# Two expert layers as seven block products, with the sums on VectorE and GpSimd and the scatters re-ordered

## The chip, the cores and the metric

The kernel runs on one core of a Trainium2 chip. The metric is device time in microseconds for one execution. TensorE (PE) multiplies and writes to PSUM; VectorE (DVE) and ScalarE (ACT) read PSUM and SBUF; GpSimd (POOL) works in SBUF and issues the indirect transfers; SyncE (SP) issues most other transfers.

## What is computed

A block of several stages on x of 4 x 512 tokens with 256 channels, all in float32. Only the first stage matters here, a mixture of experts: each token goes to the two of 8 experts that its gate ranks highest, and each expert is three matrix products.

```python
gate_w = softmax(xn @ wg_W + wg_b + (genre_embed @ gg_W + gg_b))
topk_w, topk_i = top_k(gate_w, 2)
h1 = relu(x @ W1[e] + b1[e])       # 256 -> 512
h2 = relu(h1 @ W2[e] + b2[e])      # 512 -> 512
out_e = h2 @ W3[e] + b3[e]         # 512 -> 256
moe = sum over the two experts of weight * out_e
```

The result goes through a blockwise linear attention, is added to x, and then passes a second attention and two feed-forward layers, none of which the diff touches but for one sum.

## The kernel before

**Stages.** The gate (lines 1206 to 1406) ranks the experts, counts the tokens of each and gives each token-expert pair a row in a list of slots. A slot has one expert and 256 rows (a pair of tiles) or 128 (a half slot); `SLOTS` (line 38) lists 24 of them, in the order 1,2,2 / 1,2,2 / 1,2,2,2 (three times) / 1,2,2 / 1 / 1,1, the figure being the number of 128-row tiles. The last two are inside a conditional; the other 22 (`often`, 15 pairs and 7 half slots) always run. `rowtok` holds each row's token and `goal` the row of the DRAM table `ys` where its result goes; empty rows have goal 0.

**The expert loop** (lines 1506 to 1525) does one slot j per pass, in this program order: layer 1 of slot j; the last layer of slot j - 1 (`last`, line 1477), its bias sum into `ob` and its scatters; the loads of the next slot's weights (`loads`, 1429: w1 with the biases 516 KB, w2 1 MB, w3 640 KB, double buffered); the gathers of its tokens and their transposes (`gather`, 1440, transposes at line 86 by the name `pxb`); one weight for a later stage; layer 2 of slot j. `layer` (1458) makes for each block of 128 output channels a product over 2 or 4 blocks of 128 inputs, with the 256 (or 128) tokens as the moving operand, into PSUM tiles `ph`; the relu with bias that takes them out (`relu`, 1418) goes to ACT and DVE in turn. All matmuls are issued by one helper, so they carry line 82 and are told apart by tile names: `ph` for the first two layers, `po` for the last.

**What orders the work.** A scheduler orders each engine's instructions by priority and its own estimates, and puts in all waits; instructions given to `keep_in_program_order` (`pinned`, line 1203, and `PE.in_order`) keep their order among themselves on their engine. Before the change only the transposes in `gather` are pinned in this loop, so GpSimd's other work may move in front: the sums xres + bo of the linear attention stage (line 1579, four of 128 x 1024) depend on nothing of the experts.

[...]

**After the loop** `conditions` (a small chain of another stage) fills gaps, `results` (1543) reads `ys` back, `weighted` (1554) makes y of each batch from the two expert results with ACT and then DVE (line 1558, tile `ymoe`), and `front` (1574) transposes y and begins the attention.

## Time and profile before

| | us |
|---|---|
| median of 3 runs | 1364.95 (1364.46 to 1367.05) |
| the profiled execution, its own time | 1364.1 |
| its span, first to last instruction | 1362.3 |
| expert loop in it, first layer product to last evacuation | 42.7 to 313.8 |

| in the expert loop | busy us |
|---|---|
| PE | 269.2 |
| DVE | 57.9 |
| ACT | 43.2 |
| POOL | 76.2 |

The span is what the trace covers; a run's time holds 1.8 us more around it. The profile names an operation by line, engine, and output<-input tiles. Busy time is what an engine's instructions cover, and "idle before" what it stood still ahead of them, with the instruction that ended the wait. PE is the matmul side and PEld the loading of weight blocks, which runs beside it. A float32 product shows as two records on each.

### The profile page before, as it was taken

What the parts mean: (1) busy time and instruction counts of PE and PEld (TensorE: products, weight loads), DVE (VectorE), ACT (ScalarE), POOL (GpSimd) and SP (SyncE); (2) the same over time, 40 slices, a digit from 0 to 9 for tenths busy, and PEclk for the clock granted to TensorE, in tenths of its full rate; (3) what the DMA queues carried; (4) which work ended last, traced back from release to release, by engine and by line L of the source; (5) the groups of instructions that cost most, each with busy time, mean ns of one, the idle gap of its engine ahead of it and who ended that gap; (6) DMA issues with size and microseconds to landing.
All of it is one profiled execution on the core that took longest, in us unless ns stands there. A gap on an engine that the chain in (4) does not pass through costs nothing.

```text
span 1362.3 us, 25766 instructions
## 1 busy us (share of the span) xinstructions
PE 1302.8 (96%) x10700; PEld 850.1 (62%) x10700; DVE 645.4 (47%) x1343; ACT 563.9 (41%) x1111; POOL 227.1 (17%) x223
## 2 busy tenths in 40 slices
PE   5899999998999999999999999999999998999998
PEld 4788888884666644444435665766555566667654
DVE  6222212125777743332226777764362767765421
ACT  4111111125555456565655646552223565463111
POOL 1324322211000020010103322100030312210010
PEclk7999999999999999999999999999999999999999
DMA  4577666644000000000201011211001011011000
GB/s 135 205 244 280 228 231 240 211 155 136 1 1 1 0 1 1 1 0 1 90 5 67 13 29 37 81 42 25 24 1 43 24 34 26 19 42 50 20 20 26
DMA packets 43110, 95.02 MB, mean 70 GB/s; under 512 B 9568, under 2 KB 25192, under 8 KB 40168
## 3 DMA queue, kind: packets, MB, share of 16 engines
q1 hardware_dynamic: 37560, 81.81, 18.1%
q0 software_dynamic: 3792, 10.24, 2.2%
q8 instruction: 88, 1.44, 0.4%
q10 hardware_dynamic: 1632, 1.21, 0.3%
q14 instruction: 38, 0.31, 0.1%
HBM read 83.95 MB, written 7.21 MB: 67 GB/s over the span
## 4 chain that ended last, share of the span: by engine, by line
PE 83%; DVE 7%; ACT 6%; issue 2%; DMA 1%; POOL 0%; POOLq 0%; SPq 0%; DVEq 0%; ACTq 0%
PE ph L82 14%; PE pdq L82 10%; PE sc L82 6%; PE pfy L82 6%; PE pug L82 5%; PE pua L82 5%; PE pv L82 5%; PE po L82 5%; PE pdy L82 4%; PE pn L82 3%; PE pz L82 2%; PE pds L82 2%; ACT p L685 2%; PE pqk L82 1%; PE pur L82 1%
## 5 line engine op out<-in xcount | busy, mean ns | idle before, releaser
L82 PE MATMUL pdq<-wqkv,yT 128*128 128x512 f32 x384 | 171.2, 596 | 6.0 <-ACT yT L613 4.1
L425 ACT ACTIVATE cex<-sc 128x512 f32<-128x512 f32 x256 | 131.8, 607 | 84.5 <-PE sc L82 84.4
L82 PE MATMUL ph<-h,w 128*128 128x256 f32 (+1 forms) x704 | 132.8, 346 | 1.6 <-DVE h L1422 1.6
L639 POOL TENSOR_TENSOR qr<-t,t 128x512 f32<-128x512 f32 x64 | 81.3, 1271 | 297.4 <-DVE t L636 282.8
L82 PEld LDWEIGHTS pdq<-wqkv,yT 128*128 128x128 f32 x384 | 71.4, 190 | 90.3 <-issue 76.9
L82 PEld LDWEIGHTS ph<-h,w 128*128 128x128 f32 x704 | 116.1, 191 | 13.7 <-DVE h L1422 1.9
L1420 ACT ACTIVATE h<-ph,w 128x256 f32<-128x256 f32 (+1 forms) x88 | 35.3, 437 | 190.9 <-PE ph L82 130.5
L1422 DVE TENSOR_SCALAR h<-ph,w 128x256 f32<-128x256 f32 (+1 forms) x88 | 36.1, 438 | 161.1 <-PE ph L82 102.6
L685 ACT ACTIVATE p<-pds,ss 128x192 f32<-128x192 f32 (+1 forms) x256 | 82.3, 434 | 12.5 <-PE pds L82 11.2
L82 PE MATMUL sc<-qm,kT 32*128 32x512 f32 x512 | 86.8, 639 | 0.0
L629 ACT ACTIVATE sq<-pdq 128x512 f32<-128x512 f32 x64 | 38.4, 601 | 97.1 <-POOL qr L639 50.2
L82 PE MATMUL pug<-hT,w 128*128 128x512 f32 x160 | 75.9, 597 | 0.0
L82 PE MATMUL pua<-hT,w 128*128 128x512 f32 x160 | 75.2, 592 | 0.0
L82 PE MATMUL ph<-xbT,w 128*128 128x256 f32 (+1 forms) x352 | 68.7, 347 | 0.5 <-ACT xbT L127 0.5
L82 PE MATMUL po<-w,h 128*128 128x256 f32 x296 | 67.6, 379 | 0.0
L395 POOL TENSOR_SCALAR fterm<-vw,faT 128x256 f32<-128x256 f32 x16 | 14.6, 922 | 312.1 <-DVE cr L385 259.6
L789 ACT ACTIVATE gl<-pug,cols 128x512 f32<-128x512 f32 x40 | 27.3, 687 | 86.5 <-PE pug L82 86.4
L82 PEld LDWEIGHTS ph<-xbT,w 128*128 128x128 f32 x352 | 58.5, 191 | 7.2 <-ACT xbT L127 0.7
L82 PE MATMUL pfy<-w,uA 128*128 128x256 f32 x256 | 61.2, 382 | 0.0
L82 PEld LDWEIGHTS pn<-p,v 64*64 64x64 f32 x1792 | 44.1, 136 | 27.4 <-issue 10.1
L82 PE MATMUL pv<-cex,v 128*32 128x512 f32 x512 | 61.2, 597 | 0.0
L82 PEld LDWEIGHTS po<-w,h 128*128 128x128 f32 x296 | 55.7, 190 | 8.1 <-ACT h L1420 0.9
(304 smaller groups left out, 2182.7 us busy)
## 6 DMA issues: line engine op xcount, KB each, us to landing
w<-in_moe_w_dram SPq DMA_DIRECT2D x22, 1024.0 KB
w<-in_moe_w_dram SPq DMA_DIRECT2D x22, 640.0 KB
w<-in_moe_w_dram SPq DMA_DIRECT2D x22, 516.0 KB
zb<-rows SPq DMA_DIRECT2D x32, 256.0 KB
g<-ys SPq DMA_DIRECT2D x6, 512.0 KB
wqkv<-in_f_wqkv_dram SPq DMA_DIRECT2D x2, 1536.0 KB
w<-in_f_w_dram SPq DMA_DIRECT2D x2, 1408.0 KB
out_dram<-yc SPq DMA_DIRECT2D x16, 128.0 KB
```

What stands on the lines that cost most here:

```text
L82: cls._queue(nc.tensor.matmul(*args, **kw))
L395: nc.gpsimd.tensor_scalar_mul(fterm[:, t, :], vw, W["faT"][:, t, b : b + 1])
L425: nc.scalar.activation(ex[:, i, :], pss[2 * j + i], AF.Exp, scale=CHD**-0.5)
L629: nc.scalar.activation(sq, p3, AF.Square)
L639: nc.gpsimd.tensor_tensor(qr_t[:, s], t1, t2, ALU.add)
L685: nc.scalar.activation(p[:, at : at + n], pss[j // 2][r][:, at % 384 : at % 384 + n], AF.Exp, scale=d.ss[:, j, 1, 2 * c + r : 2 * c + r + 1])
L789: nc.scalar.activation(gl, pg, AF.Gelu, bias=col("bg", l * (NU + 1) + i))
L1420: nc.scalar.activation(dst, src, AF.Relu, bias=bias)
L1422: nc.vector.tensor_scalar(dst, src, bias, 0.0, ALU.add, ALU.max)
```

## The change

For the pairs from slot 2 on (`few`, 14 of the 15), the first two layers are no longer made in eight block products. Weights, tokens and results are cut into 2 x 2 blocks; seven products of blocks or of sums of blocks (`layer_few`) give the same four result blocks after further sums, the scheme known from Strassen and Winograd. In detail:

- Each product has 128 tokens as moving operand and 256 output channels (2 matmul calls in layer 1, 4 in layer 2).
- GpSimd makes four sums of weight blocks per layer (`first_sums` of 256 columns, `second_sums` of 512), kept in the unused output tiles of the stage.
- DVE makes four sums of token blocks per layer (`token_sums`), always with one operand in PSUM: for layer 1 from the transposes' bank, for layer 2 from a second copy of h1's blocks that ACT writes into two PSUM banks (`both_banks`).
- DVE adds the products into result blocks (`plus`, seven per layer); all relus of these slots are on ACT, per 128 x 128 block.
- The slot's order changes: gathers (`fetch`) go two slots ahead; the two scatters of a pair are issued half a slot apart (the second one in the next pass, behind layer 1); nearly all instructions of the loop are pinned.
- Empty rows get a row of `ys` of their own (128 rows more, `maside`) instead of row 0, and rowtok is made ahead of goal.
- The banks are 4 `mm`, 1 `tp`, 1 `acc`, 2 for the copies; one gate product moves to `mm`.
- The sums of line 1579 are pinned, and so stay behind the scatters on GpSimd.

The diff, cut to its core (the constants' extra column, pins without other change, and the conditional slots' calls are left out):

```diff
-            moe.enter_context(banks("ps0", mm=4, tp=2, acc=2))
+            moe.enter_context(banks("ps0", mm=4, tp=1, acc=1, act=2))
...
-            ys = dr.tile([1 + 2 * B * S, H], F32, tag="ys", name="ys")
+            ys = dr.tile([1 + 2 * B * S + 128, H], F32, tag="ys", name="ys")
...
-            goal = xp.tile([128, NROWT], I32, tag="goal", name="goal")
-            nc.vector.tensor_copy(goal, pmap2[:, :NROWT])
+            goalf = xp.tile([128, NROWT], F32, tag="goalf", name="goalf")
+            nc.vector.scalar_tensor_tensor(goalf, pmap2[:, :NROWT], 0.0, maside.to_broadcast([128, NROWT]),
+                                           ALU.is_equal, ALU.mult)
+            goal = xp.tile([128, NROWT], I32, tag="goal", name="goal")
+            nc.vector.tensor_tensor(goal, pmap2[:, :NROWT], goalf, ALU.add)
...
-            def gather(j, d):
-                xb = hp.tile([128, 2, H], F32, tag="xb", name="xb", bufs=3)
+            def fetch(j, d):
+                d.xb = hp.tile([128, 2, H], F32, tag="xb", name="xb", bufs=3)
                 for i in range(d.n):
                     r = place(d.n, SLOTS[j][0]) + i
-                    nc.gpsimd.indirect_dma_start(
-                        out=xb[:, i, :], out_offset=None, in_=xall,
-                        in_offset=bass.IndirectOffsetOnAxis(ap=rowtok[:, r : r + 1], axis=0))
+                    pinned(nc.gpsimd.indirect_dma_start(
+                        out=d.xb[:, i, :], out_offset=None, in_=xall,
+                        in_offset=bass.IndirectOffsetOnAxis(ap=rowtok[:, r : r + 1], axis=0)))
+
+            def turn_tokens(d):
                 n = d.n * 128
                 pt = tpt("pxb")
-                with PE.in_order():
-                    for c in range(2):
-                        for i in range(d.n):
-                            PE.transpose(pt[:, c * n + i * 128 : c * n + (i + 1) * 128],
-                                         xb[:, i, c * 128 : (c + 1) * 128], ident)
-                xbT = hp.tile([128, 2, 256], F32, tag="xbT", name="xbT")
-                evac(xbT[:, :, 0:n], pt[:, : 2 * n].rearrange("p (c t) -> p c t", t=n))
-                d.xbT = xbT
+                for c in range(2):
+                    for i in range(d.n):
+                        PE.transpose(pt[:, c * n + i * 128 : c * n + (i + 1) * 128],
+                                     d.xb[:, i, c * 128 : (c + 1) * 128], ident)
+                d.xbT = hp.tile([128, 2, 256], F32, tag="xbT", name="xbT")
+                dst, src = d.xbT[:, :, 0:n], pt[:, : 2 * n].rearrange("p (c t) -> p c t", t=n)
+                pinned(nc.scalar.copy(dst, src))
+                if d.few:
+                    d.t1 = token_sums(d.xbT, src)
 
...
+            spare = [r.rearrange("p t h -> p (t h)") for r in y]
+            sums1 = spare[0].rearrange("p (k c m) -> p k c m", k=4, c=1)
+            sums2 = [r.rearrange("p (k c m) -> p k c m", k=2, c=2) for r in spare[1:3]]
+            sums2 = [sums2[k // 2][:, k % 2] for k in range(4)]
+
+            def first_sums(d):
+                d.s1 = [sums1[:, k] for k in range(4)]
+                weight_sums(d.s1, d.w1[:, 8:].rearrange("p (c m) -> p c m", m=ME))
+
+            def second_sums(d):
+                d.s2 = sums2
+                weight_sums(d.s2, d.w2)
+
+            def weight_sums(s, w):
+                n = w.shape[1] // 2
+                a11, a12, a21, a22 = (w[:, j0 * n : (j0 + 1) * n, 256 * i0 : 256 * i0 + 256]
+                                      for i0 in range(2) for j0 in range(2))
+                pinned(nc.gpsimd.tensor_tensor(s[0], a21, a22, ALU.add))
+                pinned(nc.gpsimd.tensor_tensor(s[1], s[0], a11, ALU.subtract))
+                pinned(nc.gpsimd.tensor_tensor(s[2], a11, a21, ALU.subtract))
+                pinned(nc.gpsimd.tensor_tensor(s[3], a12, s[1], ALU.subtract))
+
+            def token_sums(src, psum=None):
+                n = src.shape[1] // 2
+
+                def blocks(of):
+                    return [of[:, i0 * n : (i0 + 1) * n, 128 * j0 : 128 * j0 + 128]
+                            for i0 in range(2) for j0 in range(2)]
+
+                b11, b12, b21, b22 = blocks(src)
+                _, c12, c21, c22 = blocks(src if psum is None else psum)
+                if n == 1:
+                    t = hp.tile([128, 4, 1, 128], F32, tag="t1", name="t1", bufs=1)
+                else:
+                    t = spare[3].rearrange("p (k c t) -> p k c t", k=4, c=2)
+                pinned(nc.vector.tensor_tensor(t[:, 0], c12, b11, ALU.subtract))
+                pinned(nc.vector.tensor_tensor(t[:, 1], c22, t[:, 0], ALU.subtract))
+                pinned(nc.vector.tensor_tensor(t[:, 2], c22, b12, ALU.subtract))
+                pinned(nc.vector.tensor_tensor(t[:, 3], c21, t[:, 1], ALU.subtract))
+                return t
+
+            def both_banks():
+                return ps_now["pool"].tile([128, 4, 256], F32, tag="act", name="ph1", bufs=1)
+
+            def layer_few(d, src, t, tag, w, s, bias, copies=None):
+                n = w.shape[1] // 2
+                dst = hp.tile([128, 4, 256], F32, tag=tag, name=tag)
+                e1, e15, e16, e17 = (
+                    hp.tile([128, 2, 128], F32, tag=nm, name=nm, bufs=1) for nm in ("e1", "e15", "e16", "e17"))
+
+                def whole(i0, j0):
+                    return [[w[:, j0 * n + c, 256 * i0 + 128 * m : 256 * i0 + 128 * m + 128] for c in range(n)]
+                            for m in range(2)]
+
+                def summed(k):
+                    return [[s[k][:, c, 128 * m : 128 * m + 128] for c in range(n)] for m in range(2)]
+
+                def product(lhs, rhs):
+                    ps = mmt("ph")[:, :256].rearrange("p (m t) -> p m t", t=128)
+                    for m in range(2):
+                        mm(ps[:, m], [(lhs[m][c], rhs[:, c]) for c in range(n)])
+                    return ps
+
+                def block(i0, j0, out, p, other):
+                    plus(out, p, other)
+                    for m in range(2):
+                        pinned(nc.scalar.activation(
+                            dst[:, 2 * i0 + m, 128 * j0 : 128 * j0 + 128], out[:, m], AF.Relu,
+                            bias=d.w1[:, bias + 2 * i0 + m : bias + 2 * i0 + m + 1]))
+                    if copies is not None and (i0, j0) != (0, 0):
+                        for m in range(2):
+                            pinned(nc.scalar.activation(
+                                copies[:, 2 * i0 + m, 128 * j0 : 128 * j0 + 128], out[:, m], AF.Relu,
+                                bias=d.w1[:, bias + 2 * i0 + m : bias + 2 * i0 + m + 1]))
+
+                def plus(out, p, other):
+                    pinned(nc.vector.tensor_tensor(out, p, other, ALU.add))
+
+                p1 = product(whole(0, 0), src[:, 0:n, 0:128])
+                pinned(nc.scalar.copy(e1, p1))
+                p2 = product(whole(0, 1), src[:, n : 2 * n, 0:128])
+                block(0, 0, e15, p2, e1)
+                p6 = product(summed(1), t[:, 1])
+                plus(e16, p6, e1)
+                p5 = product(summed(0), t[:, 0])
+                plus(e15, p5, e16)
+                p7 = product(summed(2), t[:, 2])
+                plus(e17, p7, e16)
+                block(1, 1, e16, p5, e17)
+                p4 = product(whole(1, 1), t[:, 3])
+                block(1, 0, e1, p4, e17)
+                p3 = product(summed(3), src[:, n : 2 * n, 128:256])
+                block(0, 1, e15, p3, e15)
+                return dst
+
...
             def last(j, d):
                 ps = acct("po")
                 for i in range(d.n):
                     mm(ps[:, i * H : (i + 1) * H],
                        [(d.h2[:, c, i * 128 : (i + 1) * 128], d.w3[:, c, :]) for c in range(4)])
                 ob = hp.tile([128, 2, H], F32, tag="ob", name="ob", bufs=3)
-                nc.vector.tensor_tensor(
+                pinned(nc.vector.tensor_tensor(
                     ob[:, 0 : d.n, :], ps[:, : d.n * H].rearrange("p (i h) -> p i h", h=H),
-                    d.w3[:, 4, :].unsqueeze(1).to_broadcast([128, d.n, H]), ALU.add)
-                for i in range(d.n):
+                    d.w3[:, 4, :].unsqueeze(1).to_broadcast([128, d.n, H]), ALU.add))
+                d.ob = ob
+
+            def scatter(j, d, i):
+                if i < d.n:
                     r = place(d.n, SLOTS[j][0]) + i
-                    nc.gpsimd.indirect_dma_start(
+                    pinned(nc.gpsimd.indirect_dma_start(
                         out=ys, out_offset=bass.IndirectOffsetOnAxis(ap=goal[:, r : r + 1], axis=0),
-                        in_=ob[:, i, :], in_offset=None)
+                        in_=d.ob[:, i, :], in_offset=None))
 
 
...
-            ds = [SimpleNamespace() for _ in SLOTS]
+            ds = [SimpleNamespace(few=n == 2 and j > 1) for j, (_, n) in enumerate(SLOTS)]
+            for d, (_, d.n) in zip(ds, SLOTS):
+                pass
             loads(0, ds[0])
-            gather(0, ds[0])
+            fetch(0, ds[0])
+            fetch(1, ds[1])
+            with PE.in_order():
+                turn_tokens(ds[0])
             often, rare = ds[:-NRARE], range(len(ds) - NRARE, len(ds))
             for j, d in enumerate(often):
                 if j == len(often) - 1:
@@ -1511,18 +1620,40 @@
                     halves = nc.values_load(nhalf[0:1, 0:1], min_val=0, max_val=2 * NE)
                 if j == 1:
                     weights()
-                h1 = layer(d, d.xbT, "h1", d.w1[:, 8:].rearrange("p (c m) -> p c m", m=ME), 0)
-                if j:
-                    last(j - 1, ds[j - 1])
-                if j + 1 < len(often):
-                    loads(j + 1, ds[j + 1])
-                    gather(j + 1, ds[j + 1])
-                    if j > 1 and later:
-                        name, behind[0] = next(iter(later)), True
-                        cw_[name] = later.pop(name)()
-                        behind[0] = False
-                d.h2 = layer(d, h1, "h2", d.w2, 4)
+                w1 = d.w1[:, 8:].rearrange("p (c m) -> p c m", m=ME)
+                after = ds[j + 1] if j + 1 < len(often) else SimpleNamespace(few=False)
+                with PE.in_order():
+                    if d.few:
+                        copies = both_banks()
+                        h1 = layer_few(d, d.xbT, d.t1, "h1", w1, d.s1, 0, copies)
+                        t2 = token_sums(h1, copies)
+                    else:
+                        h1 = layer(d, d.xbT, "h1", w1, 0)
+                    if j + 1 < len(often):
+                        loads(j + 1, after)
+                        if later and j > 1:
+                            name, behind[0] = next(iter(later)), True
+                            cw_[name] = later.pop(name)()
+                            behind[0] = False
+                    if j > 1:
+                        scatter(j - 2, ds[j - 2], 1)
+                    if after.few:
+                        first_sums(after)
+                    if j + 2 < len(often):
+                        fetch(j + 2, ds[j + 2])
+                    if j:
+                        last(j - 1, ds[j - 1])
+                        scatter(j - 1, ds[j - 1], 0)
+                        if j == len(often) - 1:
+                            scatter(j - 1, ds[j - 1], 1)
+                    if j + 1 < len(often):
+                        turn_tokens(after)
+                    d.h2 = layer_few(d, h1, t2, "h2", d.w2, d.s2, 4) if d.few else layer(d, h1, "h2", d.w2, 4)
+                if after.few:
+                    second_sums(after)
             last(len(often) - 1, often[-1])
+            for i in range(2):
+                scatter(len(often) - 1, often[-1], i)
 
...
-                nc.gpsimd.tensor_tensor(
-                    xres[b], xres[b], row("bo").unsqueeze(1).to_broadcast([128, NT, H]), ALU.add)
+                pinned(nc.gpsimd.tensor_tensor(
+                    xres[b], xres[b], row("bo").unsqueeze(1).to_broadcast([128, NT, H]), ALU.add))
```

## The prediction

> **What bounds the kernel now.** First the page: is any engine full?
>
> ```profile
> span 1362.3 us, 25766 instructions
> ...
> PE 1302.8 (96%) x10700; PEld 850.1 (62%) x10700; DVE 645.4 (47%) x1343; ACT 563.9 (41%) x1111; POOL 227.1 (17%) x223
> ```
>
> TensorE is, over the whole span. The change touches the expert stage only, so next come the busy times of the stretch from its first matmul to its last evacuation (columns: sum; then PE, weight loads, DVE, ACT, POOL with counts; clock, DMA share, GB/s), and TensorE's waits there (total, times, longest).
>
> ```profile
> 42.70:313.80 271.10, 269.16 (x1441) 239.14 (x1442) 57.91 (x132) 43.18 (x102) 76.23 (x75) 1.00 0.62 217
> ```
> ```profile
> PE ph L82 <- DVE h L1422: 1.6, 1, 1.6
> PE pxb L86 <- DMA xb<-in_x_dram,rowtok: 1.2, 1, 1.2
> PE ph L82 <- ACT xbT L127: 0.5, 1, 0.5
> ```
>
> PE works 269 of 271 us at full clock and waits once each, all at the start. DVE, ACT and POOL have 200 us free. Here a matmul removed is time removed, as long as nothing new waits. The chain that ended last gives the prices (start, us, what, records):
>
> ```profile
> 106.35 8.69 PE ph L82 x48
> 115.04 3.46 PE po L82 x16
> ...
> 118.94 7.03 PE ph L82 x48
> 125.97 1.73 PE po L82 x8
> 127.69 0.44 PE pxb L86 x4
> 128.13 10.36 PE ph L82 x48
> ```
>
> Each matmul call leaves two records (a slot's last layer has 8 calls, and `po` x16). 10.36/48 = 0.216 us for 256 columns. 8.69 is 32 such records and 16 of a half slot, whose records have 128 columns: (8.69 - 32 x 0.216)/16 = 0.111; 7.03 is the reverse mix: (7.03 - 16 x 0.216)/32 = 0.112. So half the columns cost 52%.
>
> **What is saved.** A 256-row slot has 8 + 16 calls, 48 records, 10.36 us. Seven products instead of eight make 14 + 28 calls of 128 columns, 84 records x 0.1117 = 9.38 us. Saved: 0.98 us, in 14 slots (the second slot, j = 1, stays), 13.7 us. [...] The row decides: the half slots, loading full blocks for every 128 columns, take 0.112, so the loads are hidden.
>
> **What is added to GpSimd.** Rows by shape:
>
> ```profile
> L639 POOL TENSOR_TENSOR qr<-t,t 128x512 f32<-128x512 f32 x64 | 81.3, 1271 | 297.4 <-DVE t L636 282.8 <-PE pdy L82 13.5 <-PE pds L82 1.0
> L1488 POOL DMA_INDIRECT ys<-ob,goal x37 | 36.5, 987 | 101.0 <-DMA ys<-ob,goal 53.9 <-DVE ob L1483 31.5 <-issue 8.5
> ...
> L1483 DVE TENSOR_TENSOR ob<-po,w 128x256 f32<-128x256 f32 x7 | 3.0, 425 | 8.6 <-PE po L82 8.6
> ```
>
> Weight sums: 4 of 512 columns x 1.27, and 4 of 256 x 0.725 (row L396) = 8.0 us per slot. Its two gathers and two scatters, 0.98 each with 0.3 between, are 5.1. Per round of half, pair, pair, pair GpSimd has 3 x 8.0 + 7 x 2.56 = 42 us. TensorE's round, from the chain: half 9.3, first pair 12.5 - 1, later pairs 14.3 - 1 each, 47.4. So 89% full, with this order of dues: while a half slot runs (9.3 us), GpSimd needs w1 of the next slot, issued 1.2 us in and landing about 3.5 us later (1-us stretches: 300 GB/s); first sums done at 7.7, due 10.2 (its third product); two gathers and a scatter to 11.5; second sums' needed one at 14, due 16.4. They are hidden with 2 us to spare. Scatters wait for the one before (53.9 us over 16 waits in row L1488, 3.4 each); the new spacing puts 5 us of sums or gathers between them, and what was an idle queue now has sums, gathers and scatters behind each wait. I take nothing; 2 us of slack per round is the cover.
>
> **What is added to DVE and ACT, and the wait that comes of it.** DVE: 14 block sums x 0.43, token sums, about 9.5 us per slot; ACT: 22 relus and two copies, 7. Neither is full, but their chain is long: layer 2's third product needs the token sums of h1, whose first needs the last block's relu and copy. The pace of ACT and the interplay of DVE with GpSimd are read here:
>
> ```profile
> 29.59 1.06 ACT L1390 ACTIVATE ol<-ol,mc 128x64 f32<-128x64 f32 x4 [8.63 <-DVE ol L1381]
> ...
> 744.46 2.49 ACT L685 ACTIVATE p<-pds,ss 128x192 f32<-128x192 f32 x8
> ```
> ```profile
> 322.44 2.34 POOL L1579 TENSOR_TENSOR xres<-xres,crows 128x1024 f32<-128x1024 f32 x1 [5.20 <-DMA g<-ys]
> 322.84 2.62 DVE L1558 SCALAR_TENSOR_TENSOR ymoe<-g,m,g 128x256 f32<-128x256 f32 x2 [0.37 <-ACT g L1557]
> ```
> ```profile
> 1144.85 2.40 POOL L775 TENSOR_TENSOR yc<-yc,drows 128x1024 f32<-128x1024 f32 x1 [3.38 <-DVE hn L762]
> ...
> 1145.47 5.08 DVE L732 TENSOR_TENSOR oT<-oT,zb 128x512 f32<-128x512 f32 x2
> ...
> 1147.33 2.67 POOL L778 TENSOR_TENSOR yc<-yc,xres 128x1024 f32<-128x1024 f32 x1
> ```
>
> Back to back, ACT takes (1.06 - 0.34)/3 = 0.24 us for 64 columns and (2.49 - 0.43)/7 = 0.29 for 192; for 128 between them, 0.27 (it was never seen alone back to back; unpipelined it is 0.37, row L1420). From the start of layer 1 of a slot, TensorE's products end every 0.45 us, to 3.12. ACT is still in the relus of the slot before, so the first copy e1 ends at 1.65 (after a half slot 1.8, whose four relus take turns to 1.8); DVE then sums: 2.1, 2.4, 3.2 (waits for the first block's relu), 3.6, and block 11 at 4.0. From there 12 ACTs x 0.27 + 0.1 end at 7.4, two token sums x 0.43 at 8.3. TensorE's cover: 3.12, then the last layer of the slot before, 3.46 (after a half slot only 1.73), transposes 0.44, and two products of layer 2, 1.79: due at 8.8, after a half slot at 7.1. So a slot after a slot (9 cases) doesn't wait, with 0.5 spare; a slot after a half slot (5 cases: j = 4, 7, 11, 15, 19) waits 8.4 - 7.1 = 1.3. Cost 6.5 us (5.0 at pace 0.24; at 0.37 it is 2.5 x 5 and 0.6 x 9, 18 us). The output's sum, and with it the scatter, sits behind the token sums on DVE, 2.5 us later than now; its readers, GpSimd and later TensorE's bank, have that much. Four product banks: the fifth product of layer 1 needs e1 (1.65 against 1.79), the sixth block 00 (2.13 against 2.23), the seventh 2.46 against 2.68. No wait if exact, 0.2 if not: I take 0.07 x 14 = 1.0 (0 to 4).
>
> **What is moved: the residual sums.** Three of the four L1579 sums run at 127.6 to 134.6 in the expert stage, beside DVE work with a PSUM input, at no cost. Pinned, they queue behind the scatters and run right after the one shown, at 324.8 to 332. In that row two DVE operations with both inputs in SBUF take 2.62 us instead of 0.9: DVE stood still until the POOL sum ended. With two POOL sums back to back (1144.85, 1147.33), two took 5.08 instead of 1.3: one gets through per POOL sum. (Where one input is PSUM nothing happens: a DVE row at 895.66 takes its usual 0.74 beside a POOL sum. The new DVE sums all have a PSUM input, so I charge them nothing.) So the fourth ymoe piece of batch 0, on which the transposes wait, comes after the second POOL sum, 2.5 us later; batch 1's pieces then delay a copy by little. Their own readers (the tail sums, first at 395) are 60 us off. Cost 2.5 us (0 if the scheduler spreads them, 5 if batch 1's pieces hold qk's copy a full sum).
>
> The rest: goal's two operations go behind rowtok, 0.1 us gained (first used by the scatter at 58.0, made at 37; without that cover 0.4). Gathers go two slots ahead, so they wait for no transposes; on SP the loads keep their order, w3 still behind the last layer of the slot before. The regrouped gate banks are free microseconds before they are taken (the position sums' bank is last read at 26.0, taken again at 30.4; if not, some 0.3 each); conditions' small DVE chain behind busier queues at j = 21, 0 to 1, taken as 0.
>
> **Sum**, against the profiled execution (1364.1, span 1362.3, 0.85 below the median 1364.95): -13.7 + 6.5 + 1.0 + 2.5 = -3.7 us. Median 1361.2, say 1361.
>
> **Rivals.**
> - *The full saving* (20%): ACT's pace hides the token sums, or DVE and ACT overlap better; only the moved sums cost: -13.7 + 2.5 = -11, 1354. For it: the half-slot wait is only 1.3 against a chain I priced step by step. Against it: twelve ACTs on one chain.
> - *GpSimd becomes the bound* (20%): slower. Its 42 us per round meet 47.4 at a 22% higher price of a sum (1.55 us instead of 1.27), or with one scatter landing wait of 3.4 per slot. At 1.9 us a sum (12 per slot): GpSimd 54 against 47.4, 6.7 x 3 rounds plus some 3 x 2 in the shorter ones, 26 - 13.7 + 2.5 = +15, 1380; with scatter waits of 2 per slot in the full rounds only, about +3, 1368. For it: 89% leaves little, and every step waits in program order. Against it: row L639's 64 sums all take 1.27 beside a busy DVE.
> - *ACT's chain at 0.37* (12%): +18 in place of +6.5, +8, slower, 1373.
> - The change does nothing: no; 14 slots must show 128-column records.
>
> The forecast has 48%, within -7 to 0. What a measurement can tell from no change is 0.2%, 2.7 us. Faster: 20 and 33 of the 48; same: 14 of it; slower: 20 + 12 and the last 1: 53, 14, 33. Range 1353 to 1373: it leaves out the far end of the GpSimd case.
>
> **What would show it.** Right: 128x128 records at 0.112; in `ph` groups 84 records per slot; PE waits of some 1.3 us on DVE token sums just in the five slots after a half; ymoe rows stretched beside four POOL sums near 310 to 325. Wrong: PE waiting for POOL sums (the bound has moved), for DVE in every slot, or record intervals over 0.12.

## The result, and the profile after

The changed kernel takes 1378.0 us (median of 4, 1376.2 to 1378.7) where the kernel before takes 1365.5 (median of 4): 1.0085 times as long, 95% interval 1.007 to 1.010. On another chip it was 1.0102 (1.0076 to 1.0128). The forecast was 1361. In the profiled executions the span grew by 14.5 us, from 1362.3 to 1376.8.

First the head of the page.

```profile
span 1376.8 us, 27515 instructions
...
PE 1302.3 (95%) x11204; PEld 862.5 (63%) x11204; DVE 727.4 (53%) x1585; ACT 652.7 (47%) x1402; POOL 337.7 (25%) x335
```

TensorE is busy as long as before (1302.3 against 1302.8 us). Matmul work was saved and something took its place. The busy times of the expert stage (columns as before), and TensorE's waits in it:

```profile
44.66:318.68 274.02, 263.74 (x1945) 246.56 (x1946) 134.06 (x373) 131.77 (x392) 177.66 (x182) 0.99 0.64 215
```
```profile
PE ph L82 <- DVE ymoe L1519: 7.5, 10, 1.4
PE ph L82 <- ACT e L1562: 0.8, 5, 0.2
PE ph L82 <- ACT xbT L1460: 0.5, 1, 0.5
PE pcs L82 <- DVE hdT L244: 0.4, 1, 0.4
PE pfp L82 <- DVE hdT L244: 0.4, 1, 0.4
```

Before, TensorE was busy for 269.2 of 271.1 us. Now it is 263.7 of 274.0: its busy time shrank by 5.4 us. That is less than 13.7: 1.7 us of work was lost to a lower clock, and waits of a few tenths count as busy, since the profile shows a 128-column record as 0.28 us long where records start 0.11 apart. Its idle time grew from 1.9 to 10.3. The wait the forecast named, for the token sums (L1519), leads the list.

Where the 14.5 us arose, from TensorE's timelines of both profiles (each row runs from the start of the item in the row before; the pair of profiles is one execution each):

| from ... to | before, us | after, us | difference | forecast |
|---|---|---|---|---|
| start ... last layer of slot 0 | 54.2 | 54.8 | +0.6 | -0.1 |
| ... last layer of slot 19 | 234.3 | 236.2 | +1.9 | -5.6 |
| ... last layer of slot 20, with the conditions | 14.7 | 17.0 | +2.3 | -0.6 |
| ... first product of q and k | 23.5 | 25.6 | +2.1 | with the next row +2.5 |
| ... first scores of the attention stage | 14.6 | 17.9 | +3.3 | |
| ... end | 1021.0 | 1025.2 | +4.2 | 0 |

The difference runs through two things at once, idle time and clock. Summing (1 - granted clock) x TensorE's busy time over 2-us stretches gives the work lost to a reduced clock: 6.3 us in the profile before, 14.7 in the one after, so 8.4 of the 14.5. (More on this at the end: part of it is luck of these two executions.)

### The profile page after: what moved, and what is told of

Its sections match the earlier page's. It is cut to its first block, busy times and chain, and to the rows that moved or that the text cites. A ratio compares the mean times of both kernels' runs of the same rounds, so it can differ in the third digit from the quotient of the medians.

```text
span 1376.8 us, 27515 instructions
## 1 busy us (share of the span) xinstructions
PE 1302.3 (95%) x11204; PEld 862.5 (63%) x11204; DVE 727.4 (53%) x1585; ACT 652.7 (47%) x1402; POOL 337.7 (25%) x335
## 4 chain that ended last, share of the span: by engine, by line
PE 61%; DVE 6%; ACT 6%; issue 2%; DMA 1%; POOL 1%; SPq 0%; POOLq 0%; DVEq 0%; ACTq 0%
PE pdq L82 9%; PE sc L82 6%; PE pfy L82 6%; PE pug L82 5%; PE pua L82 5%; PE pv L82 5%; PE pdy L82 4%; PE pn L82 3%; PE pz L82 2%; PE pds L82 2%; ACT p L685 2%; PE pcy L82 1%; PE pck L82 1%; PE pur L82 1%; PE pcq L82 1%
## 5 line engine op out<-in xcount | busy, mean ns | idle before, releaser
L1549 ACT ACTIVATE h<-e,w 128x128 f32<-128x128 f32 x224 | 74.9, 390 | 77.6 <-DVE e L1559 77.3
L1559 DVE TENSOR_TENSOR e<-ph,e 128x256 f32<-128x256 f32 x196 | 75.1, 420 | 29.3 <-ACT h L1549 9.8
L395 POOL TENSOR_SCALAR fterm<-vw,faT 128x256 f32<-128x256 f32 x16 | 14.6, 923 | 308.3 <-DVE cr L385 255.8
L82 PE MATMUL ph<-h,w 128*128 128x128 f32 (+1 forms) x480 | 61.1, 283 | 0.0
L82 PE MATMUL pn<-p,v 64*64 64x128 f32 (+1 forms) x1792 | 50.2, 252 | 10.0 <-DVE p L688 9.1
L82 PE MATMUL pdy<-wo,oT 128*128 128x256 f32 x256 | 59.4, 383 | 0.0
L630 DVE TENSOR_REDUCE ss<-sq 128x8 f32<-128x512 f32 x64 | 43.6, 681 | 29.8 <-ACT sq L629 29.8
```

What stands on the lines that cost most here:

```text
L82: cls._queue(nc.tensor.matmul(*args, **kw))
L395: nc.gpsimd.tensor_scalar_mul(fterm[:, t, :], vw, W["faT"][:, t, b : b + 1])
L630: nc.vector.reduce_sum(ss[:, t, s, :], sq, axis=AX.X)
L1549: pinned(nc.scalar.activation(dst[:, 2 * i0 + m, 128 * j0 : 128 * j0 + 128], out[:, m], AF.Relu, bias=d.w1[:, bias + 2 * i0 + m : bias + 2 ...
L1559: pinned(nc.vector.tensor_tensor(out, p, other, ALU.add))
```

## The experiments

Ratios are to the kernel before on the same chip, with 95% intervals. No experiment leaves out or changes a part of what is computed. The theory formed from the table: the saving is real, but (a) the slots after a half lose more than they gain, (b) the held residual sums cost twice what was forecast, (c) the conditions' small matmuls now stand in a row. The rivals: the forecast's own sizes, or GpSimd as the bound.

### Is it the chain through ACT in the slots after a half?

TensorE (first fence) and ACT (second) in slot 4, the first slot after a half with seven products, in the changed kernel:

```profile
86.23 1.06 PE L82 MATMUL ph<-xbT,w 128*128 128x128 f32 x8
87.12 0.61 PE L82 MATMUL ph<-t,ymoe 128*128 128x128 f32 x4
87.90 1.16 PE L82 MATMUL ph<-t,ymoe 128*128 128x128 f32 x8 [0.17 <-ACT e L1562]
...
92.00 1.95 PE L82 MATMUL ph<-h,w 128*128 128x128 f32 x16
95.28 2.92 PE L82 MATMUL ph<-ymoe,ymoe 128*128 128x128 f32 x24 [1.33 <-DVE ymoe L1519]
```
```profile
90.31 0.69 ACT L1549 ACTIVATE h<-e,w 128x128 f32<-128x128 f32 x2 [1.28 <-DVE e L1559]
90.91 0.75 ACT L1554 ACTIVATE ph<-e,w 128x128 f32<-128x128 f32 x2
...
93.46 0.75 ACT L1554 ACTIVATE ph<-e,w 128x128 f32<-128x128 f32 x2
94.15 0.58 ACT L1460 COPY xbT<-pxb 128x512 f32<-128x512 f32 x1
94.63 0.37 ACT L1562 COPY e<-ph 128x256 f32<-128x256 f32 x1
97.41 0.69 ACT L1549 ACTIVATE h<-e,w 128x128 f32<-128x128 f32 x2 [2.41 <-DVE e L1559]
```

Twelve relus and copies run from 90.31 to 94.21, 0.325 us each, not 0.27. The token sums follow, and TensorE stands for 1.33 us. Then look at the last ACT line: layer 2's first relu comes only at 97.41, though its two products were done by 93.95. Its sum on DVE stands in program order behind the token sums, the output's sum and the next slot's token sums (94.25 to 97.04). DVE carries the delay on into the next slot.

The 0.17 us in front of 87.90 is a second wait: layer 1's fifth product wants a bank that the first copy on ACT still holds. And the last slot of each row (5, 9, 13, 17, 20), which the forecast let through without a wait, waits for its token sums too:

```profile
159.38 2.92 PE L82 MATMUL ph<-ymoe,ymoe 128*128 128x128 f32 x24 [0.25 <-DVE ymoe L1519]
```

**The seven products only where the slot before has 256 rows too**

```diff
-ds = [SimpleNamespace(few=n == 2 and j > 1) ...
+ds = [SimpleNamespace(few=n == 2 and j > 1 and SLOTS[j - 1][1] == 2) ...
```

> The changed kernel with seven products only in the nine slots that follow a 256-row slot; the five that follow a half slot keep eight. Theory: those five lose more to waits (about 2.2 us each over both layers and the slot boundary) than the 0.98 they save, so leaving them out gains 5 x 1.2 = 6 us: ratio about 1.004 beside 1.0085. Rival: the waits move to the next slot, since DVE and ACT carry their work on: no gain, 1.008.

Measured: 0.9987 (0.9972 to 1.0001), beside 1.0102 for the changed kernel on the same chip; 1365.2 us against 1367.3 before. The longest wait of this kernel for the experts' products:

```profile
PE ph L82 <- DVE ymoe L1519: 0.7, 3, 0.2
```

More than expected: the wait for token sums falls from 7.5 to 0.7 us though nine slots still have seven products. From the last layer of slot 0 to that of slot 19 it takes 228.4 us instead of 236.2. A slot whose predecessor stands behind a half now saves its share whole or nearly (from last layer to last layer 12.21 became 11.76, which saves 0.60 of 0.65; 13.93 became 13.48, 0.77 of 0.98), so part of what the five slots cost (some 2.3 us, by the same comparison slot by slot) had been booked in their followers. The theory's place is right, its extent was too small. The slots 9, 13 and 17 still wait 0.2 us each and take 12.20 as in the changed kernel: they lose by themselves.

**The order mended instead: layer 2's product of b22 third, the copies first in the last block**

```diff
 block(0, 0, e15, p2, e1)
+p3 = product(summed(3), b22)          # layer 2 only; was the last product
 p6 = product(summed(1), t[:, 1])
...
-    relus to h, then relus to the copies   # last block
+    relus to the copies, then relus to h
```

> The changed kernel with layer 2's product of b22, which needs no token sum, third instead of last, and in layer 1's last block the copies for the token sums ahead of the two relus. Theory: TensorE's waits of 1.4 us in the five slots after a half and of 0.3 in the nine others are waits for the end of the one chain through ACT; one product more of cover (0.89 us) and 0.7 us of an earlier start take all of it away, 5 x 1.4 + 9 x 0.3 = 9.7 us, the time about 1369. Rival: ACT's pace binds the whole slot, so the wait comes back at the product sums' banks or in the next slot's layer 1: -0 to -3, 1375 to 1378.

Measured: 1.0069 (1.0053 to 1.0086), 2 us better than 1.0085 where 9.7 were expected, and the two intervals overlap: near the rival. No wait for token sums is left, but others have come:

```profile
PE pxb L86 <- DMA xb<-in_x_dram,rowtok: 2.9, 2, 2.0
PE ph L82 <- ACT e L1559: 2.4, 9, 0.4
PE ph L82 <- POOL ymoe L1503: 1.7, 5, 0.6
```

In the slots themselves it gains 5.4 us (five times 13.28 became 12.82, four times 12.20 became 11.71, three times 13.93 became 13.61). The fourth weight sum, now due two products earlier, is late in the five slots after a half, the banks still wait for the first copy, and 2.9 us went to gathers that came late. So the chain was one limit of several close together.

**Seven products in layer 1 alone**

```diff
-h1 = layer_few(d, d.xbT, d.t1, "h1", w1, d.s1, 0, copies); t2 = token_sums(h1, copies)
+h1 = layer_few(d, d.xbT, d.t1, "h1", w1, d.s1, 0)
-d.h2 = layer_few(d, h1, t2, "h2", d.w2, d.s2, 4) if d.few else layer(...)
+d.h2 = layer(d, h1, "h2", d.w2, 4)
```

> The changed kernel with seven products in layer 1 alone; layer 2 has its eight again, so the copies, the token sums of h1 and the 512-column weight sums are gone, and the residual sums and conditions stay as changed. Theory: layer 2's chain through ACT eats the saving; layer 1 alone saves 28 records of 0.1117 against 16 of 0.216, 0.33 us in 14 slots = 4.6, with hardly a wait, so it is some 2 us better than the changed kernel, whose experts gave -1.9 + 3 (conditions): ratio 1.004 to 1.006. Rival: the waits come from layer 1's banks and first copy, and stay: 1.008.

Measured: 1.0043 (1.0026 to 1.006), as expected. TensorE waits for no token sum, and from slot 0's to slot 19's last layer it takes 232.7 us, 3.6 less than the changed kernel and 1.7 less than the kernel before. Slots in the middle of a row save their 0.32 whole; layer 1 of a slot after a half still loses 0.5 at its banks (11.09 against 10.92 before). So layer 2's sevenths, though worth twice as much, made the kernel slower.

### Is it GpSimd?

In the changed kernel's profile TensorE's list of waits has no weight sum (they take 1.28 us for 512 columns and 0.73 for 256, as forecast). But GpSimd's program order puts a slot's gathers behind the next slot's first weight sums, which wait for w1 (3.7 us in two waits of this profile, up to 2.1 at once). In several profiles one or two gathers land late: 2.6 us of waiting in the second run of the changed kernel, 2.9, 3.4, 4.5, 4.8 and 4.9 in others.

```diff
+if j + 2 < len(often): fetch(j + 2, ds[j + 2])
 if after.few: first_sums(after)
-if j + 2 < len(often): fetch(j + 2, ds[j + 2])
```

> The changed kernel with a slot's two gathers issued ahead of the next slot's first weight sums instead of behind them. Theory: the sums wait for w1 (2 to 3.5 us) with the gathers queued behind them, so a gather is issued 3 to 4 us before its transposes; when it lands late (6.6 us is the longest seen) TensorE waits up to 3.4 us once or twice per run, and the clock can drop after it. Ahead of the sums the gathers fit into the wait for w1: no TensorE wait for a gather but those of the first slots, the median 1 to 3 us lower (1375 to 1377), the spread of the runs smaller. Rival: the sums then come 2.6 us late and TensorE waits for GpSimd in the slots after a half: +5 and more.

Measured: 1.0082 (1.0061 to 1.0102). In its profile no gather is waited for from slot 0 on, and no sum either, so the order costs nothing; but the time doesn't differ from 1.0085 by what can be measured. The gathers are an occasional cost, not the cause.

### What do the held residual sums cost?

GpSimd (first line) and DVE behind the experts, changed kernel:

```profile
327.36 9.82 POOL L1712 TENSOR_TENSOR xres<-xres,crows 128x1024 f32<-128x1024 f32 x4 [5.83 <-PE pbusy L82]
```
```profile
326.50 0.88 DVE L1691 SCALAR_TENSOR_TENSOR ymoe<-g,m,g 128x256 f32<-128x256 f32 x2 [4.65 <-ACT g L1690]
...
327.77 4.70 DVE L1691 SCALAR_TENSOR_TENSOR ymoe<-g,m,g 128x256 f32<-128x256 f32 x2 [0.30 <-ACT g L1690]
333.89 0.69 DVE L129 COPY yT<-pt 128x512 f32<-128x512 f32 x1 [1.42 <-PE pt L86]
334.50 4.59 DVE L1691 SCALAR_TENSOR_TENSOR ymoe<-g,m,g 128x256 f32<-128x256 f32 x6
339.89 0.69 DVE L129 COPY qk<-pqk 128x512 f32<-128x512 f32 x1 [0.81 <-PE pqk L82]
```

Two pieces take 0.88 us alone and 4.70 beside the sums, as the forecast's rule said. Batch 1's six pieces take 4.59 and stand before the copy of q and k; but the copy isn't late for their sake here, since it waits 0.81 us more for TensorE. TensorE's clock in the same stretch (last columns: clock, DMA share, GB/s):

```profile
328.00:332.00 4.00, 0.33 (x1) 0.14 (x1) 4.00 (x2) 1.44 (x4) 4.00 (x2) 0.98 0.52 182
332.00:336.00 4.00, 3.48 (x8) 2.10 (x9) 2.58 (x4) 0.99 (x2) 4.00 (x3) 0.50 0.54 173
336.00:340.00 4.00, 4.00 (x8) 1.42 (x8) 3.19 (x6) 2.30 (x5) 3.13 (x3) 0.67 0.36 107
```

TensorE has 0.33 us of work in the first stretch and does much of the next ones at half clock. Its first products of q and k, before and after:

```profile
326.71 4.66 PE L82 MATMUL pqk<-yT,awqkv 128*128 128x512 f32 x8
```
```profile
333.72 6.14 PE L82 MATMUL pqk<-yT,awqkv 128*128 128x512 f32 x8
```

Between them and the first scores, 2.8 us more than before are lost to the clock, and the products behind f wait 0.5 more: the 3.3 of the table.

**That part alone, in the kernel before**

```diff
-nc.gpsimd.tensor_tensor(xres[b], xres[b], row("bo")..., ALU.add)
+pinned(nc.gpsimd.tensor_tensor(xres[b], xres[b], row("bo")..., ALU.add))
```

> The kernel before with that part alone: its four residual sums in program order behind the experts. Theory: 1365.5 + 5 to 6, about 1371 us, with four sums of 2.45 us in a row, the ymoe pieces stretched to 4.6 to 4.7 us for two and TensorE's clock at half for 3 to 7 us there. Rival (forecast's size): +2.5, 1368. If both are wrong and the sums cost nothing without the seven products: 1365.5.

Measured: 1.0045 (1.003 to 1.006), 1372.3 against 1366.3: +6 us. The pieces take 4.72 and 4.55 us there too. The theory's size holds, the forecast's 2.5 doesn't. The way differs in part: up to the first products of q and k its profile loses 2.1 us, and from there to the first scores another 2.1, mostly not by the clock (1.3 us lost there, 1.0 before) but by waits that were 0.4 us in all:

```profile
339.02 1.13 PE L82 MATMUL pf<-qk,aproj 32*128 32x512 f32 x4 [1.01 <-DVE f L1620]
341.06 1.13 PE L82 MATMUL pf<-qk,aproj 32*128 32x512 f32 x4 [0.91 <-DVE f L1620]
```

DVE makes f behind a later ymoe piece, which now waits 3.4 us for its gathered results instead of 1.6.

**Not held (the same line without `pinned`, in the changed kernel)**

> The changed kernel with the residual sums not held behind the experts any more (nothing else differs). Theory: behind the experts the four sums on GpSimd hold DVE's ymoe pieces and the first copies of the attention stage, TensorE idles there and its clock drops twice; together 5.8 us between the last expert and the steady attention stage. Then 1378.0 - 5.8, about 1372 us, two ymoe pieces back at some 2.6 us beside one sum. Rival, my forecast's size: 2.5 us, 1375.5. Second rival: three sums of 2.4 us put back among the experts take GpSimd's slack there and hold a slot's weight sums, so that the time stays within 1376 to 1379.

Measured: 1.0126 (1.0106 to 1.0146), slower: the second rival, and worse than it said. Three sums now run at 132.7 to 139.7 among the experts, in front of a slot's weight sums:

```profile
...
PE pxb L86 <- DMA xb<-in_x_dram,rowtok: 4.8, 2, 2.8
PE ph L82 <- POOL ymoe L1501: 4.4, 1, 4.4
PE pt L86 <- DVE ymoe L1691: 2.3, 1, 2.3
```

TensorE waits 4.4 us for a weight sum: here GpSimd has no room for 7 us in one piece. The late gathers (4.8 us) are in this profile too and need not come from the sums. Leaving the sums free is worse here than holding them; where to hold them is the question.

**In the last slot**

```diff
+if j == len(often) - 1:
+    for r in xres[1:] + xres[:1]:
+        pinned(nc.gpsimd.tensor_tensor(r, r, row("bo")..., ALU.add))
```

> The changed kernel with the four residual sums in GpSimd's program order inside the last slot, where it has no weight sums and DVE's inputs are mostly PSUM. Theory: GpSimd is free from about 292 to 312 and the sums (9.8 us) end before ymoe is needed; ymoe pieces are back at 2.6 us or less for two, and the 5.8 us between the last expert and steady attention are gone: 1372. Rival: the clock drops there anyway (TensorE also waits for the gathered results), so 2 to 3 us: 1375 to 1376.

Measured: 1.0086 (1.0068 to 1.0104), no gain. DVE in that slot:

```profile
312.01 5.61 DVE L256 TENSOR_SCALAR fp<-fp,fmv,frs 4x256 f32<-4x256 f32 x1
317.66 0.41 DVE L257 TENSOR_TENSOR fp<-fp,crows 4x256 f32<-4x256 f32 x1
...
318.44 0.33 DVE L1425 TENSOR_SCALAR h<-ph,w 128x128 f32<-128x128 f32 x1
```

The sums came at 308.2, behind a scatter, not at 292. One operation of the conditions on 4 rows in SBUF stood for 5.61 us beside them, and the last slot's relus behind it: TensorE waited 2.5 us for one. The cost had moved. (This profile also has 4.5 us of late gathers, which hide what else changed.)

**Spread over three slots whose next slot is a half**

```diff
+for r in {9: xres[:1], 13: xres[1:3], 17: xres[3:]}.get(j, ()):    # behind the gathers of slot j
+    pinned(nc.gpsimd.tensor_tensor(r, r, row("bo")..., ALU.add))
```

> The changed kernel with the four residual sums in GpSimd's program order in the slots before three of the half slots (one, two, one), where it has no weight sums to make and DVE's inputs come from PSUM. Theory: held behind the experts they cost some 6 us (DVE's ymoe pieces, TensorE idle, its clock): ratio 1.0085 less 0.004, 1.004 to 1.005; ymoe pieces at 1.3 us for two or less. Rival (forecast's size): 2.5 us, 1.007. Rival: TensorE waits there for the gathered results and drops its clock all the same: 1.008.

Measured: 1.0045 (1.0026 to 1.0064), 4 thousandths or 5.5 us below 1.0085 (8 us below 1.0102): the theory. There GpSimd has no weight sums to make and DVE's sums read from PSUM: beside a residual sum, slot 9 waits 0.26 us for its token sums, 0.25 without it.

### Conditions

```diff
-ps = acct("pcs")     # and acct("pfp"): one accumulator bank is left
+ps = mmt("pcs")      # and mmt("pfp"): product banks
-aside = conditions(...); next(aside)            # ahead of the last slot
+# pcs behind its layer 1, pfp behind the last layer of the slot before
```

> The changed kernel with the conditions' matmuls in three of the four product banks instead of the one remaining accumulator bank, and placed behind layer 1 and behind the last layer of the slot before, in the last slot. Theory: with one bank they stood in a row, each waiting for DVE to empty it (0.44 us twice), TensorE did little for 3 us and its clock halved over the next layers (1.7 us): 3 us gone, about 1375, and no clock below 1.0 at 304 to 308. Rival: the same small matmuls idle TensorE wherever they stand, and another drop takes the place of that one: 1378.

Measured: 1.0084 (1.0065 to 1.0102). The total shows nothing; the profile shows the part. In the changed kernel the four small pairs wait twice for DVE, and the next layer runs at half clock (0.50 from 304.6 to 308):

```profile
301.80 0.36 PE L82 MATMUL pcs<-csTc,cwe 64*128 64x4 f32 x2
302.60 0.38 PE L82 MATMUL pcs<-csTc,cwc1c 64*128 64x4 f32 x2 [0.44 <-DVE hdT L244]
302.84 0.36 PE L82 MATMUL pcs<-csTc,cwe 64*128 64x4 f32 x2
303.65 1.04 PE L82 MATMUL pfp<-cwe,hdT 128*4 128x256 f32 x4 [0.44 <-DVE hdT L244]
304.62 3.62 PE L82 MATMUL ph<-xbT,w 128*128 128x128 f32 x16
```

From the start of slot 19's last layer to that of slot 21's it takes 23.3 us before, 25.7 in the changed kernel (24.1 in its second profile, which has no clock drop there), and 22.2 with the mend, which has neither wait nor drop; a late gather in slot 4 (3.4 us) and a clock drop behind it (1.7) took the gain back in this profile. Inconclusive by time, shown by the profile: against 23.3 less slot 20's saving of 0.65, the row costs 1.4 us, 3.0 with the drop. The run changes the banks and the place together, so which of the two it is stays open.

### Is idle time the cause of the clock drops?

Idle matmuls (`busy`, read by nobody) added in the gap ahead of the ymoe transposes: four on `xres[0]`, and in a second try six on a weight tile.

```diff
-busy(2)
+busy(6)                              # first try
+PE.matmul(ps, ident, awqkv, ...)     # second try: busy(2) and six of these
```

> The changed kernel with four more idle matmuls (3.7 us) behind the experts, ahead of the ymoe transposes; nothing else differs, and their result is read by nobody. Theory: TensorE idles there for 4.4 us anyway, and the halved clock that follows costs 1.5 us in the first products of q and k and more behind it; filled with work the clock holds: 1.5 to 3 us faster, 1375 to 1376.5, no clock below 1.0 at 332 to 338. Rival: the drop isn't from idling, the matmuls are paid for: up to 2 us slower, 1380.

> The changed kernel with six idle matmuls (5.4 us, read by nobody) more ahead of the ymoe transposes, this time on a weight tile, so that the residual sums start as before. Theory: TensorE has nothing to do there until the fourth ymoe piece comes (332.5 in the changed kernel's profile); with the gap filled the clock stays whole through the first products of q and k, and 2 to 2.5 us come back there: ratio 1.007 beside 1.0085 and 1.010, and in the profile no clock below 1.0 between 330 and 340. Rival: the drop has another cause, and what is added is paid or nothing changes: 1.0085 to 1.012.

Measured: 1.0099 (1.0076 to 1.0122) and 1.0113 (1.0086 to 1.014), neither faster. In the first the residual sums waited for the added matmuls, which read `xres[0]`. In both the scheduler put the first copies of the attention stage behind more ymoe pieces (ten in a row took 12.39 us in the second), and TensorE waited 5.2 and 5.4 us for them. The clock was whole while the gap was filled and dropped with the new one: in the second it was 1.00 up to 338 and 0.50 from 340 to 346; in the first six records of q and k behind the wait took 4.59 us, where eight at a clock of 1.00 take 3.70. The drop went with the gap, but no time was won, so idle time as the cause isn't separated from the rest, and what the drops alone cost was not isolated.

### Together

**All mends in 14 slots** (gathers, conditions, third product and copies, sums in the last slot, and layer 1's first copy on DVE):

> All mends together: the gathers first, the residual sums in the last slot, the conditions in product banks, layer 2's third product that of b22, the copies first in layer 1's last block, and layer 1's first copy on DVE instead of ACT. Theory: 1378 less 5.8 (sums), 3.1 (conditions), 6 (token sum waits), 1 to 3 (gathers), and 2 to 4 of the 0.4 to 0.6 us per slot that the first copy holds layer 1's banks: 1357 to 1361, faster than both. Rival: ACT and GpSimd are so near their limit that what is taken from one wait comes back at another: 1366 to 1370.

Measured: 1.0027 (1.0015 to 1.0039). Layer 1's first copy on DVE made the slots after a half slower (13.36 against 12.82 in the run with the third product): DVE is on the chain as much as ACT.

**The changed kernel again, and all mends with that copy on ACT and the sums spread:**

> The changed kernel once more, to have it beside the next three on the same chip. If chips differ only by a common factor, its ratio to the kernel before is again 1.0085 (1.007 to 1.010). Its two sporadic costs, late gathers and where the clock drops fall, may move single runs by 3 us.

Measured: 1.0102 (1.0076 to 1.0128).

> The mends of before with layer 1's first copy back on ACT, and the four residual sums spread over three slots whose next slot is a half (no weight sums are due there). Theory: the first copy on DVE cost 0.5 us in each slot after a half and 0.1 in the others (3.7 in all), and the residual sums in the last slot held DVE there for some 2 to 3 us: 1.0027 less 0.0045, 0.998: at or below the kernel before. Rival: GpSimd's extra 2.4 to 4.7 us in those slots delays the next slot's gathers and sums: 1.002 again.

Measured: 0.999 (0.9976 to 1.0004), as expected; the same as before, not surely below it.

**Nine slots, with gathers first and conditions in product banks; then the sums spread too; then the third product too:**

> Seven products in the nine slots behind a 256-row slot, with the gathers ahead of the weight sums and the conditions in product banks; the residual sums still held behind the experts. Theory: 1.5 to 3 us less than with the nine slots alone (0.9987), from the conditions' row of waits: 0.997. Rival: the same as before, 0.9987.

> The kernel of the run above with the residual sums spread over three slots before half slots: the two differ in that alone. Theory: 4 to 6 us less than that one, 0.993 to 0.994. Rival (forecast's size): 2.5 us less, 0.995.

> The kernel of the run above with layer 2's product of b22 third and the copies first in the last block. Theory: the third slot of a row still waits 0.2 to 0.4 us before the product of the first token sum, and the slot after it at the banks; with one product more of cover 4 x 0.6 us less, 0.991 to 0.992. Rival: what is left there is the pace of DVE, in program order behind the token sums: the same as the run above.

Measured: 0.997 (0.9957 to 0.9984), 0.9931 (0.9907 to 0.9955) and 0.9937 (0.9915 to 0.9959); 1363.6, 1358.5 and 1359.9 us against 1367.6. The first two as the theory said: the sums' place is worth 5.1 us. The third is its rival by time; its profile is 1.2 us shorter in the experts (slots 9, 13 and 17 take 11.72 instead of 12.20, the slots before them 0.12 more), which these six runs can't resolve. The second kernel beats both, by 0.7% against the one before. Waits of it in the experts, and its ymoe pieces:

```profile
PE ph L82 <- DVE ymoe L1520: 0.8, 3, 0.3
...
PE po L82 <- ACT h L1424: 0.5, 1, 0.5
```
```profile
315.70 0.88 DVE L1697 SCALAR_TENSOR_TENSOR ymoe<-g,m,g 128x256 f32<-128x256 f32 x2 [2.25 <-issue]
317.44 0.69 DVE L129 COPY yT<-pt 128x512 f32<-128x512 f32 x1 [0.86 <-PE pt L86]
318.05 1.66 DVE L1697 SCALAR_TENSOR_TENSOR ymoe<-g,m,g 128x256 f32<-128x256 f32 x4
```

## Why the prediction was wrong

In the sum of the prediction, -13.7 + 6.5 + 1.0 + 2.5, the saving held. The two terms for waits and banks in the experts (7.4 us up to slot 19) measured 15.0, the moved sums (2.5) measured 5 to 6, and the conditions, put at 0, cost 1.4 or more.

- **The saving: right.** In slot 2, which nothing disturbs, records of 128 columns take 0.112 us (28 in 3.12 for layer 1, 56 in 6.30 for layer 2), and from last layer to last layer 12.37 became 11.77: 0.60 of the 0.65 that its layer 2 can save. The half slots' row (0.112 with a block loaded for every 128 columns) was the right one to go by.
- **The waits in the experts: right in kind, half in size.** This is the step that failed. The wait after a half slot was forecast as 1.3 us and is 1.33 to 1.38 in four of the five (0.76 in slot 7, where a late gather holds TensorE first). That it fits is luck: in slot 4 ACT's pace of 0.325 instead of 0.27 makes the token sums ready 8.9 us after the start of layer 1 instead of 8.4, and TensorE comes 0.6 late itself, held up by banks. What the forecast had wrong is the rest: "So a slot after a slot (9 cases) doesn't wait, with 0.5 spare", and "I take 0.07 x 14" for the banks. The losses up to slot 19, from the starts in TensorE's timeline:

| us lost up to slot 19 | forecast | measured |
|---|---|---|
| before layer 2's third product, slots after a half | 6.5 | 7.0 |
| the same, slots after a slot (0.2 or 0.4 in seven of eight) | 0 | 2.3 |
| in layer 1, at the banks (0.43 after a half, 0.39 in slots 9, 13 and 17, 0.1 to 0.3 in others) | 0.9 | 4.1 |
| layer 2's later products | 0 | 0.9 |
| a late gather | 0 | 0.6 |

Where the trace names what layer 1 waited for, it is the first copy on a busy ACT. The rows make 15.0 us (14.9 as rounded) instead of 7.4, against a saving of 13.1, and turn the forecast's -5.6 into +1.9. Of it some 2.3 us is delay that DVE and ACT, in program order, carry from the slots after a half into their followers: it went when those slots got their eight products back. The forecast priced one wait at the first product that meets it, and not what was queued behind it.
- **The residual sums: mechanism right, size wrong.** Forecast 2.5, measured 6.0 alone in the kernel before, 5.5 and 5.1 when taken out. The 2.5 for batch 0's fourth piece is there (24.4 us from slot 20's last layer to the end of that wait, 21.9 before). What failed is "batch 1's pieces then delay a copy by little": what followed cost as much again, in the changed kernel's profile by a half clock that the forecast had no term for (2.8 of 3.3 us), in the kernel before with held sums mostly by products that waited for DVE's f.
- **Conditions "taken as 0": wrong.** 1.4 us, 3 with the clock drop. The forecast looked at DVE's queue. In the changed kernel `pcs`, `pcs` and `pfp` share one accumulator bank with the last layers, and stand in a row where the kernel before had layer 1's products between them; the mend undid both at once.
- **The gate and goal: about right.** The +0.6 at slot 0's last layer isn't the change's: x landed later in that execution (TensorE waits 2.1 us for it), with a clock drop behind it (0.50 from 12 to 14 us), and the kernel before lost 1.6 us there to a relu. In other profiles slot 0's last layer starts at 52.6 to 54.7 us, in the kernel before with held sums at 52.6.
- **GpSimd: not the bound, as forecast**, but its order had less room than "2 us to spare" said: gathers wait behind sums that wait for w1, and 7 us in one piece among the experts cost 4.4 at once.
- **The rival that came nearest** is the slow side, ACT's chain, with 18 us of waits where 15.0 came. Its 18 rested on a pace of 0.37 that wasn't there, so this is luck too.
- **Left open:** +1.9, +0.7 for the conditions' row and 5.5 for the sums make 8 of the 12.5 us. The rest isn't settled; late gathers and the clock are candidates. The last 4.2 us of the table, where all engines have the same instructions in the same order, are not shown to be the change's. That stretch took 1026.4 us in the kernel before with held sums, 1026.2 in the second profile of the changed kernel and 1021.8 in the best one, with 3.3 to 6.6 us of work lost to the clock (1.7 in the first profile of the kernel before).

## What to carry to other kernels

When a change puts a long chain on engines that run in program order, price not only the first wait but everything queued behind it on each engine, up to where the queue is empty again. A saving per tile is best taken only where the tile before leaves the cover; nine of fourteen here gave more than all. Work moved to an engine for its free time needs a place where no other engine's operands are in its way, found in the trace: of four places for the same four sums, three cost 5 us or more against the fourth.

## What the runs showed of the hardware

**A GpSimd sum on SBUF held up DVE operations that had all their operands in SBUF, small ones too.** One on four rows of 256 took 5.61 us beside sums of 128x1024, where its neighbour took 0.41; ten of 128x256 took 12.39 (0.44 each alone). A DVE sum with one operand in PSUM took its usual 0.42 us at 94.25 in the changed kernel, beside a weight sum on GpSimd.

**The clock dropped in or behind idle stretches of TensorE, but not at each.** At one place both kernels have the same waits, 2.0 us in all, yet (first fence before, second after; third number from the right is the clock):

```profile
708.00:712.00 4.00, 2.79 (x18) 2.19 (x18) 2.12 (x5) 0.00 (x0) 0.00 (x0) 1.00 0.00 0
```
```profile
719.00:723.00 4.00, 2.79 (x14) 2.30 (x13) 2.12 (x5) 0.00 (x0) 0.00 (x0) 0.74 0.00 0
723.00:727.00 4.00, 3.99 (x18) 3.17 (x16) 1.03 (x2) 0.00 (x0) 0.00 (x0) 0.83 0.00 0
```

This drop is at 0.50 from 720.9 to 724.3, 3.4 us, and costs 1.7 us of work; the one behind the residual sums lasts twice as long, and costs 3.1. Another, from 304.6 to 308, came behind two waits of 0.44 us among the conditions' small matmuls, and cost 1.7. What sets a drop off no run shows: the waits ahead of the drop at 720.9 are 0.8 and 1.2 us with transposes between them, TensorE was busy for 2.79 of the 4 us shown, and the same waits have a drop in one execution and none in the other.

It makes single profiles poor witnesses: over 98 executions of the kernel before on five occasions, those with a mean clock of 0.992 took 1364.1 us (5 of them), those with 0.985 1370.6 (6), so 0.9 us per thousandth. The ten executions of the changed kernel have 0.985 in the mean, the kernel before about 0.988: by this estimate some 3 of the 12.5 us go with the clock, less than the 8.4 of the two profiles. That its longer gaps cause this is likely, but only argued.
